# Other start addresses in SBUF for the split weights, half of x's blocks and the down weights

## The chip, the cores and the metric

The kernel runs on one core of a Trainium2 chip. The metric is the device time of one execution in microseconds. The kernel before was run three times: 998.46, 1000.0 and 1001.24 us, median 1000.0. A further execution was taken with the hardware profiler; every profile line below comes from it.

## The reference

One decoder-like block: cross attention onto a context, then a mixture of eight experts in which every expert is computed for every token. All is float32. Biases of the attention are drawn at random, so they can't be dropped.

```python
# x (16,112,256), ctx (16,375,256), Wq/Wk/Wv (256,256)
q = layernorm(x) @ Wq + bq;  k = ctx @ Wk + bk;  v = ctx @ Wv + bv
x = x + softmax(q @ k.T / 16) @ v
n = layernorm(x)                                  # 1792 tokens of 256
cw = softmax(n @ w_router) * softmax(n @ w_gating / 0.1)
cw = cw / (cw.sum(-1) + 1e-9)                     # (tokens, 8)
for e in range(8):                                # w_gate, w_up (8,256,1024), w_down (8,1024,256)
    h = silu(n @ w_gate[e]) * (n @ w_up[e])
    x = x + cw[:, e] * (h @ w_down[e])
```

## The kernel before

**Attention, then experts.** The first part, some 125 us, computes attention batch by batch in a software pipeline (attn_group, attn_batch, tick). Its result lies transposed in x1T (two halves of 896 tokens). From then on almost all time goes to the experts, in 128 steps, one for each of 8 experts, 2 token halves h, 4 column groups j and gate or up (the list steps, L440). The order of instructions on TensorE, VectorE, ScalarE and GpSimd is the order in which the program writes them down; nothing reorders it.

**Products.** A gate or up step multiplies a 2 x 2 block matrix of x with a 2 x 2 block matrix of the weight by seven products instead of eight (PROD, L20: the Strassen-Winograd scheme). x's seven combinations are made once per half (xs_hi and xs_lo, L121 and L122, each block 128 partitions x 448 float32r, 1792 bytes in a partition); the weight's seven are made for each step. Full float32 precision is kept by splitting every operand into a high part that float32r holds exactly and a low part. A product is then three passes (PASSES, L79): high x high, high weight x low x, low weight x high x. Function prod (L573) issues these three matmuls. The weight block is the stationary operand, which TensorE loads before the matmul; x's block is the moving operand, which streams through. The products go to the PSUM banks A, B, C and E, and VectorE combines them (L684 to L729).

**Split weights.** A step's weight is fetched by the SP queue into a raw buffer (load_raw), combined by GpSimd (load_t), rounded by ScalarE into the high half of a w buffer (load_hi, L486), and GpSimd subtracts to get the low half (load_lo, L491). A w buffer holds 2 x 7 blocks of 128 float32r, 7168 bytes in a partition, which is 28 x 256. There are eight w buffers. In the attention part the same buffers hold x, parts of the context and x1T (wide, L132).

**Down products.** The hidden values of a half are split too, into hhi and hlo (four buffers each of 3584 bytes), and multiplied with w_down: in down_group (L531) a block of the hidden values is stationary and the down weight is moving, 256 columns, again in three passes: hhi with the high weight, hhi with the low weight, hlo with the high weight. Down weights come through rawd into four buffers d (load_d, L493), each 4096 bytes: a high and a low half of 2 x 256. Function fill puts down groups between the products of the following steps, so TensorE always has one of the two at hand. gather adds finished groups to acc with the routing weight.

**Addresses.** All these tiles are taken in turn from two pools; a tile starts at the next multiple of 32 bytes. Function buf (L106) takes all rotating buffers; AHEAD (L104) puts a small unused tile ahead of the first buffer of some tags and so shifts where these start. The starts in the built program, modulo 256 bytes:

| tile | role in the experts | start modulo 256 |
|---|---|---|
| xs_hi, xs_lo | moving, products | 192 (all 28 blocks) |
| w, every block of all 8 buffers | stationary, products | 128 |
| d, all 4 buffers | moving, down products | 0 |
| hhi / hlo | stationary, down products | 64 / 192 |

All blocks inside these tiles begin at multiples of 256 bytes from the tile's start (448 x 4 = 7 x 256; 128 x 4 = 2 x 256), so a tile's residue is that of each of its operands.

The names that return below: L578 is the matmul of a product, L544 that of a down group, L276, L305, L332 and L342 are matmuls of the attention.

Of the kernel before, what the change touches and what calls it, by code (L numbers as in the profile page):

```python
# [8 lines left out]
F32 = mybir.dt.float32  # L9
FR = mybir.dt.float32r  # L10
# [21 lines left out]
def kernel(  # L32
# [18 lines left out]
    P = 128  # L51
    B, TQ, D = x.shape
# [9 lines left out]
    NH = 2  # L62
    HT = NT // NH
    HB = B // NH
    N = HT // 2
# [5 lines left out]
    cpool = ctx.enter_context(tc.tile_pool(name="const", bufs=1))  # L71
    fpool = ctx.enter_context(tc.tile_pool(name="ffn", bufs=2))
# [28 lines left out]
    BUFS = {"w": 8, "d": 4, "hhi": 4, "hlo": 4, "s": 11, "v1": 2, "raw": 3, "rawd": 2, "tt": 2, "y": 3}  # L101


    AHEAD = {"w": 16, "d": 32, "hhi": 16, "hlo": 32}  # L104

    def buf(tag, shape, name, dtype=F32):  # L106
        if tag in AHEAD:
            fpool.tile([P, AHEAD.pop(tag)], F32, tag=f"ahead_{tag}", name=f"ahead_{tag}", bufs=1)
        return fpool.tile(shape, dtype, tag=tag, name=name, bufs=BUFS[tag])

    zero = buf("y", [P, 256], "zero")
    nc.vector.memset(zero, 0.0)
    zero = zero.bitcast(mybir.dt.bfloat16)
# [4 lines left out]
    warm = cpool.tile([P, G], F32, name="warm")  # L118
    nc.scalar.activation(warm, nhalf, AF.Exp)

    xs_hi = [[cpool.tile([P, N], FR, name=f"xs_hi{h}{i}") for i in range(7)] for h in range(NH)]  # L121
    xs_lo = [[cpool.tile([P, N], FR, name=f"xs_lo{h}{i}") for i in range(7)] for h in range(NH)]  # L122
    pairs = [(h, b, min(2, NTT - 2 * b)) for h in range(NH) for b in range((NTT + 1) // 2)]
    accs = {(h, b): cpool.tile([P, n, D], F32, name=f"acc{h}{b}") for h, b, n in pairs}
    acc = [accs[h, b][:, i, :] for h, b, n in pairs for i in range(n)]
# [4 lines left out]

    WF = 2 * 7 * P
    wide = [buf("w", [P, WF], f"wide{i}") for i in range(7)]  # L132
    qk_b = [wide[0][:, i * KC * GT : (i + 1) * KC * GT] for i in range(2)]
    late = [wide[i] for i in (3, 1, 2)]
# [4 lines left out]
    x1T = [wide[5 + h].rearrange("p (k t) -> p k t", k=KC) for h in range(NH)]  # L139

    wn = buf("d", [P, 2, KC, D], "wn")
    wT = buf("d", [P, 2, KC, D], "wT")
    wv_b = buf("d", [P, 2, KC, D], "wv_b", FR)
# [3 lines left out]
    b_b = buf("rawd", [P, 2, D], "b_b")  # L147
    wv = buf("rawd", [P, KC, D], "wv")
    bk_c = spool.tile([P, KC], F32, tag="bk_c", name="bk_c", bufs=1)
    junk = cpool.tile([P, D], F32, name="junk")  # L150
    bkb = buf("y", [P, D], "bkb").rearrange("p (k q) -> p k q", k=KC)

    xg = {}
# [351 lines left out]
    for k in range(NW):  # L505
        e, i = divmod(k, PER)
        if e == 0:
            n = i - 2
            plan(n - 1, "raw", k)
        else:  # L510
            n = 2 * PER * (e - 1) + PER + (2, 4, 6, 7, 8, 10, 12, 13)[i]
# [4 lines left out]
    for q in range(E * NJ):  # L516
        e, j = divmod(q, NJ)
        n = 2 * j + 1 if e == 0 else 2 * PER * (e - 1) + PER + 2 * j + 7
# [393 lines left out]
```

## Time and profile before

| what | value |
|---|---|
| median of three runs | 1000.0 us (998.46 to 1001.24) |
| the profiled execution | 1002.6 us |
| its span, from the first to the last instruction | 1000.8 us |
| mean granted TensorE clock | 0.986 of full speed |
| matmuls of products (L578) / of down groups (L544) | 2688 / 2688 |
| SBUF bytes of one partition used by the last tile's end | 228668 |

The profile page gives busy time by engine, a chain of work followed back from the last instruction, and groups of equal instructions. "PE" is TensorE's matmuls, "PEld" its loads of stationary operands, "DVE" VectorE, "ACT" ScalarE, "POOL" GpSimd. A matmul's duration on the page reaches from its start to its modelled end; matmuls are pipelined and overlap, so the time that one costs is read from the start of one to the start of the next in the view in order of time. In that view the columns are start in us, length of the merged entry in us, engine, line, operation, out<-in by names, shape, and how many instructions were merged.

### The profile page before, as it was taken

To read this page: it belongs to the slowest core of one execution; us is meant where nothing else is said; L and a number is where in the kernel's file an instruction comes from. 1 tells how busy PE (TensorE), PEld (TensorE's weight loads), DVE (VectorE), ACT (ScalarE), POOL (GpSimd) and SP (SyncE) were. 2 spreads that over 40 slices of the span, in tenths; PEclk is the share of its full clock that TensorE was granted. 3 is DMA by queue.
4 is the path that set the end of the run, shared out by engine and by line. 5 is a ranking of instruction groups with operands and counts; after the bars stand their busy time and mean duration, and the time that the engine had idled before them with its cause. 6 is when DMAs were issued, how large, how long until landed. Compare 5 with 4: busy or idle time off the path is not lost.

```text
span 1000.8 us, 16367 instructions
## 1 busy us (share of the span) xinstructions
PE 978.5 (98%) x6052; PEld 911.8 (91%) x6052; DVE 802.9 (80%) x1529; ACT 496.1 (50%) x1036; POOL 419.4 (42%) x548
## 2 busy tenths in 40 slices
PE   7989889999999999999999999999999999999998
PEld 4867778999999999999999999999999999999998
DVE  5875668888888888878888888888887888788786
ACT  4554664445545554455444553555444554455342
POOL 2352765245615462255414460555235632445000
PEclk9999979999999999999999999999999999999999
DMA  9710111001100110011100110011001110010011
GB/s 222 208 29 14 41 47 53 11 23 53 40 14 22 44 34 31 12 28 48 43 2 23 53 54 1 22 44 43 22 12 42 37 40 11 22 43 2 1 38 38
DMA packets 36736, 39.06 MB, mean 39 GB/s; under 512 B 3552, under 2 KB 34656, under 8 KB 36656
## 3 DMA queue, kind: packets, MB, share of 16 engines
q1 hardware_dynamic: 36384, 37.76, 13.0%
q8 instruction: 47, 0.77, 0.3%
q14 instruction: 33, 0.27, 0.1%
q10 hardware_dynamic: 272, 0.26, 0.1%
HBM read 34.34 MB, written 1.84 MB: 36 GB/s over the span
## 4 chain that ended last, share of the span: by engine, by line
PE 93%; DVE 2%; DMA 2%; ACT 1%; POOL 0%; issue 0%; SPq 0%; DVEq 0%
PE pd L544 32%; PE pC L578 16%; PE pA L578 15%; PE pB L578 15%; PE pE L578 8%; PE ps_s L305 2%; PE ps_aT L332 1%; PE ps_o L342 1%; DMA wide<-in_x_dram 1%; PE ps_qk L276 1%; PE ps_lg L406 1%; DMA ctx<-in_ctx_dram 1%; PE ps_cT L298 1%; PE ps_pT L323 0%; ACT xs_hi L380 0%; PE ps_x1T L369 0%
## 5 line engine op out<-in xcount | busy, mean ns | idle before, releaser
L544 PE MATMUL pd<-wd,hhi 128*128 128x256 f32 x1792 | 338.8, 280 | 0.0
L544 PEld LDWEIGHTS pd<-wd,hhi 128*128 128x128 f32 x1792 | 308.9, 188 | 14.1
L544 PE MATMUL pd<-wd,hlo 128*128 128x256 f32 x896 | 250.6, 280 | 0.0
L578 PE MATMUL pC<-xs_hi,w 128*128 128x448 f32 x512 | 189.7, 370 | 0.8 <-DVE s_3c L707 0.8
L578 PE MATMUL pB<-xs_hi,w 128*128 128x448 f32 x512 | 188.6, 368 | 0.0
L578 PE MATMUL pA<-xs_hi,w 128*128 128x448 f32 x512 | 187.4, 366 | 0.9 <-ACT v L679 0.4
L544 PEld LDWEIGHTS pd<-wd,hlo 128*128 128x128 f32 x896 | 169.3, 189 | 0.0
L561 POOL TENSOR_TENSOR acc<-acc,y 128x256 f32<-128x256 f32 x45 | 35.9, 824 | 247.5 <-ACT y L560 247.5
L491 POOL TENSOR_TENSOR w<-raw,w 128x384 fp32r<-128x384 f32 x64 | 73.2, 1144 | 136.1 <-ACT w L486 136.1
L679 ACT COPY v<-pA 128x448 f32<-128x448 f32 x128 | 68.2, 533 | 92.2 <-PE pA L578 92.2
L578 PEld LDWEIGHTS pC<-xs_hi,w 128*128 128x128 f32 x512 | 96.8, 189 | 11.3 <-DVE s_3c L707 1.1
L578 PEld LDWEIGHTS pB<-xs_hi,w 128*128 128x128 f32 x512 | 97.1, 190 | 5.6
L578 PEld LDWEIGHTS pA<-xs_hi,w 128*128 128x128 f32 x512 | 96.6, 189 | 5.9 <-ACT v L679 1.0
L578 PE MATMUL pC<-xs_lo,w 128*128 128x448 f32 x256 | 93.6, 366 | 0.0
L578 PE MATMUL pE<-xs_hi,w 128*128 128x448 f32 x256 | 93.4, 365 | 0.0
L578 PE MATMUL pB<-xs_lo,w 128*128 128x448 f32 x256 | 93.1, 364 | 0.0
L578 PE MATMUL pA<-xs_lo,w 128*128 128x448 f32 x256 | 92.7, 362 | 0.0
L491 POOL TENSOR_TENSOR w<-tt,w 128x512 fp32r<-128x512 f32 x64 | 83.5, 1304 | 2.1
L496 POOL TENSOR_TENSOR wd<-rawd,wd 128x512 fp32r<-128x512 f32 x32 | 41.7, 1302 | 72.6 <-ACT wd L495 72.6
L578 PEld LDWEIGHTS pE<-xs_hi,w 128*128 128x128 f32 x256 | 48.2, 188 | 3.2
L578 PEld LDWEIGHTS pC<-xs_lo,w 128*128 128x128 f32 x256 | 48.5, 189 | 1.5
L578 PEld LDWEIGHTS pB<-xs_lo,w 128*128 128x128 f32 x256 | 48.3, 189 | 1.7
(1779 smaller groups left out, 1887.4 us busy)
## 6 DMA issues: line engine op xcount, KB each, us to landing
raw<-in_L_ffn_w_gate_dram SPq DMA_DIRECT2D x32, 256.0 KB, 3.3
raw<-in_L_ffn_w_up_dram SPq DMA_DIRECT2D x32, 256.0 KB, 2.7
rawd<-in_L_ffn_w_down_dram SPq DMA_DIRECT2D x32, 256.0 KB, 2.6
ctx<-in_ctx_dram SPq DMA_DIRECT2D x13, 336.0 KB, 6.8
wide<-in_x_dram SPq DMA_DIRECT2D x4, 448.0 KB, 4.0
out_dram<-acc SPq DMA_DIRECT2D x6, 256.0 KB, 2.2
wide<-in_ctx_dram SPq DMA_DIRECT2D x3, 336.0 KB, 7.0
ctx<-in_ctx_dram SPq DMA_DIRECT2D x13, 39.0 KB
```

The lines of the kernel that those rows point to most:

```text
L276: nc.tensor.matmul(ps, m_sb[:, k, m * P : (m + 1) * P], xnT[:, k, :], start=(k == 0), stop=(k == KC - 1),)
L298: nc.tensor.transpose(ps[:, c * KT : (c + 1) * KT], ct[:, c, k * P : (k + 1) * P], ident[:KT, :KT])
L305: nc.tensor.matmul(sc, qkT[g][:, k, i * TQ : (i + 1) * TQ], ctT[k], start=(k == 0), stop=(k == KC - 1),)
L332: nc.tensor.matmul(ps[:, k, :], ct[:, c, k * P : (k + 1) * P], pT[:, c, :], start=(c == 0), stop=(c == NK - 1),)
L342: nc.tensor.matmul(po, aT[:, a, k, :], (wv_hi, wv_lo)[w][:, k, :], start=(k == 0 and s == 0), stop=(k == KC - 1 and s == 2),)
L406: nc.tensor.matmul(ps[:, j, :], x1T[h][:, k, j * P : (j + 1) * P], wr[:, k, :], start=(k == 0), stop=(k == KC - 1),)
L491: nc.gpsimd.tensor_sub(wts[k][1][:, d], w, f(wts[k][0][:, d]))
L496: nc.gpsimd.tensor_sub(t[:, 1], rawds[q], f(t[:, 0]))
L544: nc.tensor.matmul(pd, hs[a][:, t * P : (t + 1) * P], wds[q][w][:, fi, :], start=(opening and s == 0), stop=(last and s == 2), skip_group_ ...
L561: nc.gpsimd.tensor_add(acc[tt], acc[tt], y)
L578: nc.tensor.matmul(ps, w_[w][:, wi, :], (xs_hi, xs_lo)[a][h][xi], start=(start and s == 0), stop=(stop and s == 2), skip_group_check=True,)
L679: nc.scalar.copy(v1, pa)
```

## The change

Only addresses change. Buffers of tag w are taken 8 elements (32 bytes) longer and used from element 4 (16 bytes) on; with the length of 7200 bytes each next buffer starts 32 bytes further modulo 256. Buffers of tag d are taken 16 elements (64 bytes) longer. AHEAD is set so that the eight used w starts are 16, 48, 80, 112, 144, 176, 208 and 240, and the four d starts 0, 64, 128 and 192 modulo 256. x's blocks are now taken half by half, with an unused tile of 32 bytes ahead of the second half: 192 for half 0, 224 for half 1. The starts of hhi and hlo stay at 64 and 192. To have room, the scratch tile junk goes; what is written there goes to the last block of acc, which is filled later. acc, cw, wr and the y buffers move by 32 bytes as a consequence.

```diff
-    AHEAD = {"w": 16, "d": 32, "hhi": 16, "hlo": 32}
+    AHEAD = {"w": 40, "d": 0, "hhi": 16, "hlo": 32}
+    LONGER = {"w": (8, 4), "d": (16, 0)}

     def buf(tag, shape, name, dtype=F32):
-        if tag in AHEAD:
+        if AHEAD.get(tag):
             fpool.tile([P, AHEAD.pop(tag)], F32, tag=f"ahead_{tag}", name=f"ahead_{tag}", bufs=1)
-        return fpool.tile(shape, dtype, tag=tag, name=name, bufs=BUFS[tag])
+        if tag not in LONGER:
+            return fpool.tile(shape, dtype, tag=tag, name=name, bufs=BUFS[tag])
+        n = 1
+        for d in shape[1:]:
+            n *= d
+        more, first = LONGER[tag]
+        t = fpool.tile([shape[0], n + more], dtype, tag=tag, name=name, bufs=BUFS[tag])[:, first : first + n]
+        if len(shape) == 3:
+            return t.rearrange("p (a b) -> p a b", a=shape[1])
+        if len(shape) == 4:
+            return t.rearrange("p (a b c) -> p a b c", a=shape[1], b=shape[2])
+        return t
...
-    xs_hi = [[cpool.tile([P, N], FR, name=f"xs_hi{h}{i}") for i in range(7)] for h in range(NH)]
-    xs_lo = [[cpool.tile([P, N], FR, name=f"xs_lo{h}{i}") for i in range(7)] for h in range(NH)]
+    xs_hi, xs_lo = [], []
+    for h in range(NH):
+        if h:
+            cpool.tile([P, 8], F32, name="ahead_x")
+        xs_hi.append([cpool.tile([P, N], FR, name=f"xs_hi{h}{i}") for i in range(7)])
+        xs_lo.append([cpool.tile([P, N], FR, name=f"xs_lo{h}{i}") for i in range(7)])
...
-    junk = cpool.tile([P, D], F32, name="junk")
+    junk = acc[-1]
```

## The prediction

> **What bounds the kernel now.** I read the page's busy shares first, then its chain, then the stretches by engine, then TensorE's instructions in order of time.
>
> ```profile
> PE 978.5 (98%) x6052; PEld 911.8 (91%) x6052; DVE 802.9 (80%) x1529; ACT 496.1 (50%) x1036; POOL 419.4 (42%) x548
> PE 93%; DVE 2%; DMA 2%; ACT 1%; POOL 0%; issue 0%; SPq 0%; DVEq 0%
> ```
>
> The chain that ended last is 93% TensorE. The stretches (columns: PE busy, weight loads, VectorE, ScalarE, GpSimd, granted clock, DMA share, GB/s) say it more sharply:
>
> ```profile
> 250.00:500.00 250.00, 250.00 (x1560) 237.88 (x1559) 207.41 (x355) 126.85 (x250) 113.50 (x139) 1.00 0.11 31
> 500.00:750.00 250.00, 250.00 (x1561) 238.13 (x1560) 207.42 (x357) 123.40 (x243) 101.45 (x126) 1.00 0.09 27
> ```
>
> From 250 to 985 us TensorE is never idle, the clock is 1.00, and the view of waits lists nothing for it. So only the length of a matmul itself can move the time. In order of time, one gate or up step runs from one first product to the next:
>
> ```profile
> 504.66 0.36 PE L578 MATMUL pA<-xs_hi,w 128*128 128x448 f32 x1
> ...
> 506.81 0.36 PE L578 MATMUL pA<-xs_hi,w 128*128 128x448 f32 x1
> 507.01 0.36 PE L578 MATMUL pA<-xs_lo,w 128*128 128x448 f32 x1
> 507.21 0.36 PE L578 MATMUL pA<-xs_hi,w 128*128 128x448 f32 x1
> 507.41 0.36 PE L578 MATMUL pE<-xs_hi,w 128*128 128x448 f32 x1
> ...
> 508.01 0.40 PE L544 MATMUL pd<-wd,hhi 128*128 128x256 f32 x2
> 508.25 0.28 PE L544 MATMUL pd<-wd,hlo 128*128 128x256 f32 x1
> 508.36 0.40 PE L544 MATMUL pd<-wd,hhi 128*128 128x256 f32 x2
> ...
> 511.37 0.36 PE L578 MATMUL pA<-xs_hi,w 128*128 128x448 f32 x1
> ```
>
> Durations overlap, so the starts count. A step is 511.37 - 504.66 = 6.71 us: 21 product matmuls (448 columns, one every 0.20 us) and 21 down matmuls (256 columns, three in 0.35 us). Over 250 to 985 us the means of the start-to-start times are 201.7 ns (26 hiccups over 240 ns left out) and 118.0 ns; 21 x 201.7 + 21 x 118.0 = 6.71 us. Two lines of the attention stage give floors:
>
> ```profile
> 90.86 1.67 PE L276 MATMUL ps_qk<-wide,mix 128*128 128x448 f32 x4
> 69.47 1.50 PE L332 MATMUL ps_aT<-pT,wide 125*128 125x112 f32 x12
> ```
>
> ps_qk streams plain float32 at half rate: (1.67 - 0.54)/3 = 377 ns for 448 columns, so about 188 ns at the full rate of the float32r products (estimate: half). ps_aT streams so few columns that its weight loads set the pace: (1.50 - 0.28)/11 = 111 ns per load. The products therefore carry 201.7 - 188 = 13.7 ns each over the floor, the down matmuls 118.0 - 111 = 7 ns over the weight load. With 2688 of each that is 37 + 19 = 56 us in which TensorE is busy but neither waits for an engine nor streams at its own rate.
>
> That excess hangs on addresses and on phase, not on other engines. Of 110 steps that start after 250 us, 97 last 6.713 us within 2 ns, whatever VectorE, ScalarE, GpSimd and the DMAs do meanwhile; the other 13 are 0.2 us longer. Within a step the product intervals repeat by position: 200.8 ns for the first pass of most products, 197.5 for their second, on xs_lo, 209.2 for the last pass of pB's second product. All of these have the same start residues modulo 256: moving x at 192, stationary w at 128. The down matmuls (moving 0) take 117.3 ns when a hidden block at 64 is loaded next and 119.4 when one at 192 is.
>
> **What the Trainium skill says.** "TensorE: Matmul & The Clock Gate", section "Back-to-back issue gap", gives N / 2.4 + 2.5 ns. For two passes over 448 columns that is 375.8 ns, and ps_qk agrees (377); for float32r it would be 189 and 109 ns, and the trace disagrees (201.7, 118.0). "SBUF — State Buffer", section "Who interferes with whom", gives TensorE two independent read ports and says it never waits on anyone; the 56 us above speak against taking this as free. The same page's box on cachelines ("Door 1: The DMA port swizzle") names 16-byte lines, so a shift by 16 bytes changes lines; and "Operand start alignment" says its own findings are about legality, not speed. No run here shows a start at an odd multiple of 16.
>
> **The change, part by part.** In the built program all engines issue the same instructions in the same order with the same semaphore waits; only addresses differ, and the 19 VectorE instructions that wrote junk write acc[-1] instead. So nothing is queued behind anything new.
>
> - *Split weights* (w) go from residue 128 in all eight buffers to 16, 48, 80 ... 240; *x* stays at 192 in half 0 and goes to 224 in half 1. The distance w minus x, one value now (192 modulo 256) wherever a w block is loaded while x streams, becomes eight values, the odd multiples of 16. The trace holds no such distance, so I bound it. Best case: all excess goes, 2688 x 13.7 = 37 us less. Worst case: every product takes the longest interval seen, 209.2, so 2688 x 7.5 = 20 us more. The value taken: the present single distance is a special one (whole multiples of 64 on both sides, so both streams cross line and block borders in step, and a meeting repeats), and mixing should bring the mean to about the best common interval that is seen now, 198. That is 3.6 ns x 2688 = 9.7 us less.
> - *Down weights* (d) go from residue 0 to 0, 64, 128, 192 against hidden blocks still at 64 and 192. Both hidden kinds then see all four distances. ps_o, the attention matmul of this form (256 columns, moving at 0), has medians of 115.5 to 117 ns at distances 0, 64 and 128, beside 118.0 here. I take 0.5 ns less, 2688 x 0.5 = 1.3 us; bounds: all at the 111 floor (19 us less) or all at 122, the slow end seen (11 us more).
> - *Other engines.* ScalarE (L486) and GpSimd (L491, 1.14 and 1.30 us) write w off 32-byte borders. Cover: GpSimd is 42% busy and idles 136 us before L491 for ScalarE; a tenth slower would cost it 16 us of idle time and TensorE nothing. If that cover went, the first product of a step would wait for its low part. VectorE's tiles acc and y shift by 32 bytes: nothing taken.
> - *Start-up.* The first x load (4.12 us, first on the chain) lands in a w buffer, now 16 bytes off. Bound: 0 to twice its time, 4 us more. I take 0.
> - *junk to acc[-1]*: the same engine in the same order, and acc[-1] is filled long after: 0.
>
> Sum: -9.7 - 1.3 = -11.0 us. The profiled execution lasted 1002.6 us (span 1000.8), so 991.6; it lies 2.6 above the median of the three runs, 1000.0, so against that median 989 us.
>
> **Rivals.**
> 1. *Large gain:* an offset of half a 32-byte pair keeps the two read streams apart throughout. Two thirds of the products' excess and a fifth of the downs' go: 24.6 + 3.8 = 28 us, 972 us. For it: the excess is large and follows addresses only. Against: the weight load advances at another rate than the moving stream (111 ns for 128 columns, 188 for 448), so a start offset alone can't part them for good.
> 2. *No difference:* because the streams drift past each other, start residues average out and intervals stay near 201 and 118: 998 to 1003 us. For it: the down matmuls differ by only 2 ns between distances 64 and 192. Against: the same drift repeats to the ns in 97 steps, so starts do decide.
> 3. *Slower:* blocks that start inside a 64-byte unit touch one unit more per weight load and, in half 1, per moving row, and meet more often. It decides once the products' mean is 1.1 ns up (3 us). At half of the way to the longest interval seen (+3.5 ns) it costs 9.4 us: 1009 us. For it: the present layout puts x, w and both hidden kinds on distinct multiples of 64, which may be a good point already. Against: the products carry more excess than anything else, so that point isn't good for them.
> 4. *It doesn't do what it says:* excluded; the built addresses have the residues named.
>
> **How the numbers follow.** Main case 0.55 (own range 979 to 996), rival 1 0.15, rival 2 0.12, rival 3 0.18. Half of rival 1 falls below 972, and rather over half of rival 3 above 1008, about 0.17 together: the range is 972 to 1008. A measurement of this kernel can tell about 0.3%, 3 us. Faster: main and rival 1 less the shallow end of the main case, 0.69; same: 0.12 and a little of the main case and rival 3, 0.14; slower: 0.17.
>
> **What would show it.** Right: product intervals near 198 ns, a step length that now differs from step to step and repeats with the eight weight buffers, TensorE still without waits between 250 and 985 us, the start of the first pass of the experts unmoved. Down intervals near 117.5, differing with the d buffer. Wrong: product intervals above 202 (rival 3), intervals unchanged (rival 2), or TensorE waiting for VectorE, 80% busy now, if TensorE gains so much that it runs ahead (the 13 longer steps would then grow). If the attention stage alone moved, my reading of where the addresses act would be wrong.

## The result and the profile after

| | before | after |
|---|---|---|
| median of five runs | 1001.24 us (998.46 to 1002.89) | 1005.59 us (1004.88 to 1007.59) |
| profiled execution / its span | 1002.6 / 1000.8 us | 1005.97 / 1004.2 us |
| first product starts at (from the trace's start times) | 112.7 us | 112.7 us |
| mean start to start, product / down matmul, 250 to 985 us | 201.73 / 118.04 ns | 203.76 / 117.76 ns |
| steps without a wait (95 after 250 us in each) | 6.713 to 6.714 us | 6.711 to 6.787 us |

After over before, worked out from all five executions of each, is 1.0051, with a 95% interval of 1.0031 to 1.0071: the change makes the kernel 0.5% slower. (The two medians alone give 1.0043.) The means and step lengths here and below are worked out from the start times of the trace; product intervals above 240 ns, which hold a wait, are left out of the means.

The busy shares on the page of the changed kernel:

```profile
PE 982.0 (98%) x6052; PEld 910.9 (91%) x6052; DVE 804.1 (80%) x1529; ACT 496.0 (49%) x1036; POOL 419.8 (42%) x548
```

The instruction counts and the shares of the chain (93% TensorE) are those of before; only TensorE's busy time grew, by 3.5 us, and the span by 3.4. The stretches of the changed kernel (columns as before: PE, weight loads, VectorE, ScalarE, GpSimd, clock, DMA share, GB/s):

```profile
250.00:500.00 250.00, 250.00 (x1554) 236.73 (x1553) 207.43 (x353) 126.09 (x250) 113.66 (x139) 1.00 0.10 31
500.00:750.00 250.00, 250.00 (x1555) 236.86 (x1554) 206.41 (x354) 122.40 (x241) 101.55 (x125) 1.00 0.09 27
```

By its busy time TensorE is still never idle, at a clock of 1.00, but it starts 1554 and 1555 matmuls where it started 1560 and 1561. Busy time can't show this loss; only the count and the start times do. One step of the changed kernel, in order of time (half 1, x at 224, w at 48):

```profile
505.80 0.37 PE L595 MATMUL pA<-xs_hi,w 128*128 128x448 f32 x1
...
508.18 0.37 PE L595 MATMUL pA<-xs_lo,w 128*128 128x448 f32 x1
508.39 0.37 PE L595 MATMUL pA<-xs_hi,w 128*128 128x448 f32 x1
508.59 0.37 PE L595 MATMUL pE<-xs_hi,w 128*128 128x448 f32 x1
...
509.20 0.40 PE L561 MATMUL pd<-wd,hhi 128*128 128x256 f32 x2
...
509.56 0.40 PE L561 MATMUL pd<-wd,hhi 128*128 128x256 f32 x2
...
510.27 0.36 PE L595 MATMUL pB<-xs_hi,w 128*128 128x448 f32 x1
...
512.54 0.37 PE L595 MATMUL pA<-xs_hi,w 128*128 128x448 f32 x1
```

L595 and L561 are the old L578 and L544. The step is 512.54 - 505.80 = 6.74 us. Step lengths now repeat with period 16, the eight w buffers times the two halves. Product matmuls start 0.20 or 0.21 us after one another, where they started 0.20 us apart.

In 13 of the steps TensorE does wait, before and after. The busy time of its matmuls hides it; the waits of its weight loads (PEld) show it. At pC's first product the load waits for the VectorE instruction that reads bank C (the source line c12 = w16 + pc). The view has 13 such lines for each kernel between 250 and 985 us (us in total, times, longest); one of before and the same one of after:

```profile
PEld pC L578 <- DVE s_63w L729: 0.3, 1, 0.3
PEld pC L595 <- DVE s_63w L746: 0.2, 1, 0.2
```

The account of the change: products 2.03 ns x 2688 = +5.5 us; down matmuls -0.28 x 2688 = -0.8; the excess of the product intervals over 240 ns, all at such a wait, falls from 2.4 us (26 of them) to 1.2 (13), -1.2. Together that is +3.5 us, beside +3.4 in the spans.

### The profile page after: what moved, and what is told of

The parts are those of the page before. It is cut to its first block, busy times and chain, and to the rows that moved or that the text cites. A ratio compares the mean times of both kernels' runs of the same rounds, so it can differ in the third digit from the quotient of the medians.

```text
span 1004.2 us, 16367 instructions
## 1 busy us (share of the span) xinstructions
PE 982.0 (98%) x6052; PEld 910.9 (91%) x6052; DVE 804.1 (80%) x1529; ACT 496.0 (49%) x1036; POOL 419.8 (42%) x548
## 4 chain that ended last, share of the span: by engine, by line
PE 93%; DVE 2%; DMA 2%; ACT 1%; POOL 0%; issue 0%; SPq 0%; DVEq 0%
PE pd L561 31%; PE pC L595 16%; PE pA L595 16%; PE pB L595 15%; PE pE L595 8%; PE ps_s L322 2%; PE ps_aT L349 1%; PE ps_o L359 1%; DMA wide<-in_x_dram 1%; PE ps_qk L293 1%; PE ps_lg L423 1%; DMA ctx<-in_ctx_dram 1%; PE ps_cT L315 1%; PE ps_pT L340 0%; ACT xs_hi L397 0%; PE ps_x1T L386 0%
## 5 line engine op out<-in xcount | busy, mean ns | idle before, releaser
L561 PE MATMUL pd<-wd,hhi 128*128 128x256 f32 x1792 | 338.9, 280 | 0.0
L561 PEld LDWEIGHTS pd<-wd,hhi 128*128 128x128 f32 x1792 | 308.5, 188 | 15.8
L561 PE MATMUL pd<-wd,hlo 128*128 128x256 f32 x896 | 250.9, 280 | 0.0
L595 PE MATMUL pC<-xs_hi,w 128*128 128x448 f32 x512 | 189.8, 371 | 0.8 <-DVE s_3c L724 0.8
L595 PE MATMUL pA<-xs_hi,w 128*128 128x448 f32 x512 | 189.1, 369 | 0.7 <-ACT v L696 0.4
L595 PE MATMUL pB<-xs_hi,w 128*128 128x448 f32 x512 | 188.0, 367 | 0.0
L561 PEld LDWEIGHTS pd<-wd,hlo 128*128 128x128 f32 x896 | 168.7, 188 | 0.1
L578 POOL TENSOR_TENSOR acc<-acc,y 128x256 f32<-128x256 f32 x45 | 36.1, 831 | 249.2 <-ACT y L577 249.2
L508 POOL TENSOR_TENSOR w<-raw,w 128x384 fp32r<-128x384 f32 x64 | 73.2, 1144 | 136.7 <-ACT w L503 136.7
L595 PEld LDWEIGHTS pC<-xs_hi,w 128*128 128x128 f32 x512 | 96.9, 189 | 10.8 <-DVE s_3c L724 1.1
L595 PEld LDWEIGHTS pA<-xs_hi,w 128*128 128x128 f32 x512 | 96.9, 189 | 6.3 <-ACT v L696 1.0
L595 PEld LDWEIGHTS pB<-xs_hi,w 128*128 128x128 f32 x512 | 96.8, 189 | 6.1
L595 PE MATMUL pB<-xs_lo,w 128*128 128x448 f32 x256 | 94.1, 368 | 0.0
L595 PE MATMUL pA<-xs_lo,w 128*128 128x448 f32 x256 | 94.1, 368 | 0.0
L595 PE MATMUL pC<-xs_lo,w 128*128 128x448 f32 x256 | 94.1, 367 | 0.0
L595 PE MATMUL pE<-xs_hi,w 128*128 128x448 f32 x256 | 93.7, 366 | 0.0
L508 POOL TENSOR_TENSOR w<-tt,w 128x512 fp32r<-128x512 f32 x64 | 83.0, 1297 | 2.8
L595 PEld LDWEIGHTS pE<-xs_hi,w 128*128 128x128 f32 x256 | 48.2, 188 | 4.2
L595 PEld LDWEIGHTS pB<-xs_lo,w 128*128 128x128 f32 x256 | 48.3, 189 | 2.1
L595 PEld LDWEIGHTS pC<-xs_lo,w 128*128 128x128 f32 x256 | 48.4, 189 | 1.8
```

What stands on the lines that cost most here:

```text
L508: nc.gpsimd.tensor_sub(wts[k][1][:, d], w, f(wts[k][0][:, d]))
L561: nc.tensor.matmul(pd, hs[a][:, t * P : (t + 1) * P], wds[q][w][:, fi, :], start=(opening and s == 0), stop=(last and s == 2), skip_group_ ...
L578: nc.gpsimd.tensor_add(acc[tt], acc[tt], y)
L595: nc.tensor.matmul(ps, w_[w][:, wi, :], (xs_hi, xs_lo)[a][h][xi], start=(start and s == 0), stop=(stop and s == 2), skip_group_check=True,)
```

## The experiments

A product's **distance** below is the start of the stationary block that is loaded next minus the start of the moving block, modulo 256. All nine full kernels are the changed one with other values of AHEAD and LONGER, and with x at 192 throughout unless x is named. For x at 192 the unused tile ahead of the second half goes, with the line `if h:` over it, which the cuts below leave out. Every ratio is to the kernel before on the same chip and is worked out from all executions, so it can differ from the ratio of the medians by up to 0.1%. The means in ns are of one profiled execution each.

| kernel | w; d; hhi/hlo | ratio [95%] | product, down ns | first-order change, us |
|---|---|---|---|---|
| before | 128; 0; 64/192 | 1 | 201.73, 118.04 | |
| after | odd multiples of 16, x 192 and 224; 0, 64, 128, 192; 64/192 | 1.0051 [1.0031, 1.0071] | 203.76, 117.76 | +5.5 - 0.8 |
| w_alone | odd multiples of 16; 0; 64/192 | 1.0015 [1.0005, 1.0025] | 203.92, 116.72 | +5.9 - 3.5 |
| d_alone | 128; 0, 64, 128, 192; 64/192 | 0.9987 [0.9975, 1.0] | 201.45, 117.56 | -0.8 - 1.3 |
| x_alone | 128, x 192 and 224; 0; 64/192 | 1.001 [0.9997, 1.0024] | 202.77, 117.08 | +2.8 - 2.6 |
| w_spread_32 | multiples of 32; 0; 64/192 | 1.0021 [1.0011, 1.0031] | 203.55, 117.43 | +4.9 - 1.6 |
| w_at_96 | 96; 0; 64/192 | 0.9974 [0.9965, 0.9984] | 203.90, 115.19 | +5.8 - 7.7 |
| best_distances | 128; 64; 128/128 | 0.999 [0.998, 0.9999] | 201.19, 118.03 | -1.5 - 0.0 |
| hlo_at_64 | 128; 0; 64/64 | 0.9917 [0.9894, 0.994] | 200.49, 115.41 | -3.3 - 7.1 |
| best_step | 128; 192; 128/128 | 0.9894 [0.9875, 0.9913] | 200.03, 114.87 | -4.6 - 8.5 |
| best_step_b | 128; 192; 128/0 | 0.9838 [0.9814, 0.9862] | 200.04, 113.37 | -4.5 - 12.6 |

The last column is the difference of each mean to before, times 2688; it leaves out the waits.

**The three parts alone.** w_alone leaves out the shift of x and the spread of d:

```diff
-    AHEAD = {"w": 40, "d": 0, "hhi": 16, "hlo": 32}
-    LONGER = {"w": (8, 4), "d": (16, 0)}
+    AHEAD = {"w": 48, "d": 0, "hhi": 16, "hlo": 32}
+    LONGER = {"w": (8, 4)}
-            cpool.tile([P, 8], F32, name="ahead_x")
```

> The kernel before with the eight w buffers at 16, 48 ... 240 modulo 256 (the residue of each buffer as in the changed kernel); x stays at 192, d at 0, hidden blocks at 64 and 192. Theory A, the products became slower because of w's new starts: product intervals 203.5 to 204 ns (201.7 before), down intervals 118.0, step mean 6.76 us, 4 to 6 us over the kernel before. Theory B, the new starts of x or d, or the mixture of all, did it: product intervals within 0.5 ns of 201.7 and the time within 1.5 us of the kernel before.

The products rose by 2.19 ns, about as much as under the whole change, as theory A said. The down matmuls, whose own addresses are those of before, fell by 1.32 ns, which neither theory had: what a down matmul costs depends on what ran before it too. So the kernel became only 0.15% slower, 1.5 us where theory A had 4 to 6.

d_alone spreads only d:

```diff
+    AHEAD = {"w": 16, "d": 32, "hhi": 16, "hlo": 32}
+    LONGER = {"d": (16, 0)}
-            cpool.tile([P, 8], F32, name="ahead_x")
```

> The kernel before with the four d buffers at 0, 64, 128, 192; w at 128, x at 192 as before. Theory A: product intervals 201.7 ns as before, down intervals 117.5 to 117.8 (118.0 before), 0.5 to 1.5 us less than the kernel before. Theory B, that moving d upsets the products that follow the downs: product intervals 202.5 ns or more, 2 us or more slower.

The kernel became 0.13% faster, at the edge of what can be told, as theory A said; the down matmuls fell by 0.48 ns. This part alone isn't what cost time.

x_alone moves only x's second half:

```diff
+    AHEAD = {"w": 8, "d": 32, "hhi": 16, "hlo": 32}
+    LONGER = {}
```

> The kernel before with x's second half at 224 instead of 192; w at 128, d at 0. Theory A, start residues average out in the products unless w moves: steps of half 1 as long as those of half 0, 6.71 us, no change in time. Theory B, the 32 bytes of x matter: steps of half 1 differ from those of half 0 by 0.03 us or more (64 such steps: 2 us or more).

The two halves make a comparison inside one execution. From product to product the interval is 201.03 ns in half 0 (distance 192) and 204.05 ns in half 1 (distance 160); the stationary blocks are the same. Yet a step of half 1 lasts 6.720 us against 6.713, since the down matmuls fell again. Theory A is wrong about the products, and theory B's 0.03 us a step didn't come; the time is that of before within its interval.

The parts don't add up. Alone they cost 0.15%, -0.13% and 0.10%, together 0.12%; the whole change costs 0.51%. By the last column they give +0.5 us together against +4.7. The products' rise is there with w alone, but the fall of the down matmuls that comes with it (-3.5 us with w alone) is nearly lost when all three move (-0.8).

**TensorE by itself.** streams has no other work than matmuls on one moving and one stationary tile. Here go issues ten matmuls of N columns with the moving block at m and the stationary block at s; cols is the number of stationary columns:

```diff
+MOV = (0, 32, 64, 128, 192)
+STAT = tuple(range(0, 256, 16))
...
+    for N in (448, 256):
+        for m in MOV:
+            for s in STAT:
+                go(N, m, s)
+    for cols in (128, 64, 32):
+        for m, s in ((192, 128), (192, 16), (0, 64), (0, 0)):
+            go(448, m, s, cols, 16)
...
```

> Nothing of the reference is computed: TensorE alone runs float32r matmuls back to back, ten of each kind, with 448 and 256 moving columns, the moving start at 0, 32, 64, 128, 192 and the stationary start at every multiple of 16 modulo 256; then the same with 128, 64 and 32 stationary columns. Theory A, two reading streams that drift past each other: all 80 cells for 448 columns lie within 196 to 210 ns, with no distance below 194, and with 32 stationary columns the interval falls to about 190. Theory B, a distance that keeps the streams apart exists: some cells near 189 while others are over 205, in a pattern by stationary minus moving start. Theory C, the excess comes from other engines: every cell near 189.

Intervals for 448 columns with the moving block at 0, from the start times; each is the mean of the last seven of a group's nine:

```
distance   0     16    32    48    64    80    96    112
ns       203.3 206.6 204.6 203.6 201.7 203.6 200.1 203.6
distance  128   144   160   176   192   208   224   240
ns       202.7 202.4 205.7 204.4 200.1 203.9 206.6 203.4
```

Only the distance counts: with the moving block elsewhere the values belong to the same distances within 1.2 ns. All 80 groups lie between 199.6 and 206.7 ns, in theory A's range; nothing is near 189, so the excess neither comes from other engines (theory C) nor goes away at some distance (theory B). The 192 of the kernel before is, with 96, the lowest value. The mean over the odd multiples of 16, which the change spreads the products over, is 203.9 ns; the changed kernel's mean is 203.76. And 160 against 192, which x_alone saw as 204.05 against 201.03, is here 205.7 against 200.1. So the table gives the direction, but not the size: the products took 201.73 ns before, not 200.1, and it is partly luck that 203.76 meets the table so closely. With 256 columns the groups span 113.3 to 120.7 ns, and there one distance can settle at two values: 192 takes 117.7 ns with the moving block at 0 and 113.4 with it at 128. One part of theory A missed: with 32 stationary columns the 448-column interval stays at 202 to 206 ns. So the excess isn't the length of the weight load, though that changes which distance is low (192 takes 205.8 ns with 32 stationary columns).

**Is it the start off 32 bytes?** w_spread_32 puts the buffers at all multiples of 32:

```diff
+    AHEAD = {"w": 48, "d": 0, "hhi": 16, "hlo": 32}
+    LONGER = {"w": (8, 0)}
-            cpool.tile([P, 8], F32, name="ahead_x")
```

> Only w is moved: the eight buffers at 0, 32, 64 ... 224, so no start is off 32 bytes. Theory A2, each product costs what its distance (stationary minus moving start, modulo 256) costs in the table of the bare streams, and only the mean over the distances counts: the table's mean over the multiples of 32 is 203.1 ns, so product intervals 202.5 to 203.6, between the kernel before (201.7) and w alone on odd multiples of 16 (203.9). Theory B2, starts off 32 bytes are what costs: product intervals 201.7 or less, as before.

It costs as much as w_alone, with no block off a 32-byte border. The mean of the table over multiples of 32 is 203.1 ns; the products took 203.55, in theory A2's range. So it isn't the odd 16 bytes that cost.

**Do the distances add up?** w_at_96 gives all products one distance that isn't among the low ones (96 - 192 = 160), which by the table alone makes the kernel slower:

```diff
+    AHEAD = {"w": 8, "d": 40, "hhi": 16, "hlo": 32}
+    LONGER = {}
-            cpool.tile([P, 8], F32, name="ahead_x")
```

> Only w is moved, all eight buffers together from 128 to 96, so the common distance to x becomes 160 instead of 192. Theory A2: the table has 205.7 ns there against 200.1, so product intervals rise to 204 to 206 and the kernel takes 6 to 11 us more, twice the change's loss, though no buffer differs from another. Theory B2, that it is the mixture of distances or the odd multiples of 16 that costs: no change, 201.7.

The products took 203.90 ns, just under the forecast 204 to 206, with no mixture and no odd 16 bytes: a single other distance costs the products as much as the spread over eight. But the time forecast missed: the kernel became faster, by 2.8 us. In order of time (w_at_96; L559 is the down matmul, L593 the product):

```profile
500.12 0.39 PE L559 MATMUL pd<-wd,hhi 128*128 128x256 f32 x2
...
500.46 0.39 PE L559 MATMUL pd<-wd,hhi 128*128 128x256 f32 x2
...
504.21 0.37 PE L593 MATMUL pB<-xs_lo,w 128*128 128x448 f32 x1
504.42 0.37 PE L593 MATMUL pB<-xs_hi,w 128*128 128x448 f32 x1
```

The products are slower, 0.21 us here. But three down matmuls take 0.34 us instead of the 0.35 of before, though d, hhi and hlo stand where they stood before: -7.7 us against +5.8. hlo_at_64 changes nothing but hlo's start:

```diff
+    AHEAD = {"w": 16, "d": 32, "hhi": 16, "hlo": 0}
+    LONGER = {}
-            cpool.tile([P, 8], F32, name="ahead_x")
```

> Only hlo is moved, from 192 to 64, so all hidden blocks lie 64 past d. Theory A2: the table has 113.3 ns for 256 columns at distance 64, so down intervals fall from 118.0 to 113.5 to 115, products stay at 201.7, 8 to 12 us less. Theory C2, that the downs keep drifting through several patterns because products stand between them: down intervals 116.5 to 118, less than 4 us gained.

The kernel became 0.8% faster, 8.3 us, with steps of 6.633 us. The gain is theory A2's, but only part of the reason is: the down matmuls took 115.41 ns, just above its range, and the products, which it left at 201.7, fell to 200.49. best_distances takes for each pair the distance that the table calls best:

```diff
+    AHEAD = {"w": 16, "d": 48, "hhi": 16, "hlo": 0}
+    LONGER = {}
-            cpool.tile([P, 8], F32, name="ahead_x")
```

> x 192, w 128 as before; d 64, both hidden kinds 128: every pair that meets has a distance with the table's lowest value (w on x and hidden on x 192: 200.1 ns; hidden on d and w on d 64: 113.3). Theory A2: products 200.1 to 201, downs 113.5 to 114.5, step 6.60 to 6.63 us, 985 to 989 us. Theory C2: downs 116 or more, 994 us or more.

The forecast gain of 12 to 16 us didn't come: the time is that of before within 0.1%, and the down matmuls took 118.03 ns, as before. A table of steady pairs doesn't price a mixed sequence.

**The whole step, by itself.** steps issues the kernel's 42 matmuls of a step in their order, on tiles with given starts, with nothing else running. A layout in CONFIGS is the starts of w, d, hhi and hlo with x at 0. Each is issued three times (REPS), 256 layouts in multiples of 64 among them:

```diff
+    def step(W, D, *H):
+        prod("A", 1, True, False, W)
+        prod("B", 6, True, True, W)
+        prod("C", 5, True, False, W)
+        down(D, H)
...
+    for c in CONFIGS:
+        for _ in range(REPS):
+            step(*c)
```

> Nothing of the reference is computed. TensorE alone issues a step's 42 matmuls (21 product passes, 21 down passes, in the kernel's order and shapes) three times for each of many choices of the starts of w, d, hhi and hlo against x; no other engine works and nothing waits. First four choices: the distances of the kernel before, of hlo at 64, of the best distances, of w at 96. Theory D, TensorE's own streams set every interval and the step as a whole falls into a fixed pattern: the third repeat takes 6.713, 6.633, 6.703 and 6.700 us within 0.01, as in the full kernels. Theory E, other engines' SBUF traffic carries part of it: steps here are 0.05 us or more shorter, and the order of the four differs. Ahead of that, 448 and other column counts with 128 and 32 stationary columns[...]; and plain float32 at 448 columns, 376 ns at every start if the half rate leaves room for both streams.

In their second and third repeats the bare steps of the layouts of before, hlo_at_64, best_distances and w_at_96 last 6.713, 6.633, 6.702 to 6.706, and 6.700 to 6.701 us. In the full kernels they last 6.713, 6.633, 6.701 to 6.705, and 6.700. The trace of steps in order of time, first a step with the starts of the kernel before, then one with the best found:

```profile
201.70 0.76 PE L72 MATMUL A<-xs,w 128*128 128x448 f32 x3
...
205.05 1.22 PE L72 MATMUL D<-d,h 128*128 128x256 f32 x9
206.11 0.78 PE L72 MATMUL B<-xs,w 128*128 128x448 f32 x3
...
208.41 0.76 PE L72 MATMUL A<-xs,w 128*128 128x448 f32 x3
...
4425.09 0.76 PE L72 MATMUL A<-xs,w 128*128 128x448 f32 x3
...
4428.43 1.18 PE L72 MATMUL D<-d,h 128*128 128x256 f32 x9
4429.45 0.76 PE L72 MATMUL B<-xs,w 128*128 128x448 f32 x3
...
4431.67 0.76 PE L72 MATMUL A<-xs,w 128*128 128x448 f32 x3
```

The first step takes 6.71 us and the second 6.58, and nine down matmuls take 1.06 us and 1.02. At the third repeat the 256 layouts go from 6.580 to 6.836 us with a mean of 6.729: the kernel before already stood a little better than the mean. (30 of the 256 still change by more than 5 ns from the second repeat to the third.) The same run swept the columns. With 32 stationary columns 128 moving columns take 60 ns and 512 take 232, so each further column costs 0.45 ns. A plain float32 matmul leaves two records in the trace; each took 375.9 ns for 448 columns, 0.84 ns a column, at all 16 distances. At this half rate the addresses don't matter.

steps_mix does the same for the changed kernel: 16 successive steps with its own starts. An entry of MIX is w, x, d for each of the step's seven down groups, and (hhi, hlo), on the scale where x of half 0 is 0:

```diff
+    MIX = [(112, 0, [0, 0, 0, 0, 0, 0, 128], (128, 0)), ...]
+    for _ in range(3):
+        for c in MIX:
+            mixed(*c)
```

> Nothing of the reference is computed. TensorE alone issues sixteen consecutive steps of the changed kernel, each matmul with the start residues that it has there, three times over; then more choices of uniform starts at multiples of 32 and 16. Theory D: the second and third pass show the step lengths of the changed kernel's profile, step by step, between 6.71 and 6.80 us with a mean near 6.755 (the two steps of sixteen that also wait there left out). Theory E: the lengths differ from the changed kernel's, or are all near 6.71.

Bare steps of the second pass in ns, and below them the changed kernel's own, from 451.6 us on, in the same order:

```
bare    6715  6744 6751 6759 6743 6772 6748  6768 6745 6787 6772 6711 6729 6770 6751 6769
kernel  6795* 6744 6751 6759 6743 6772 6848* 6768 6745 6787 6772 6711 6729 6770 6751 6769
```

The starred steps hold a wait for VectorE; the other 14 agree to the ns. The step shown above of the changed kernel, here bare (trace of steps_mix in order of time):

```profile
184.89 0.78 PE L73 MATMUL A<-xs,w 128*128 128x448 f32 x3
...
188.30 1.23 PE L73 MATMUL D<-d,h 128*128 128x256 f32 x9
189.37 0.77 PE L73 MATMUL B<-xs,w 128*128 128x448 f32 x3
...
191.64 0.57 PE L73 MATMUL A<-xs,w 128*128 128x448 f32 x2
```

Here the down groups, B and the next A come 3.41, 4.48 and 6.75 us after the first A. In the changed kernel they come 3.40, 4.47 and 6.74 us after 505.80. The bare mean of 6.752 us against 6.713 is 0.039 us, times 128 steps +5.0 us: that is the products' and down matmuls' share of the loss (5.5 - 0.8 = 4.7), made by TensorE alone. Between the bare steps only the starts of its two operands differ.

The same run tried 220 more choices of uniform starts, in multiples of 16 and 32; none was shorter than 6.580 us.

**Better than both.** best_step takes the 6.580 us layout in which hhi and hlo start alike:

```diff
+    AHEAD = {"w": 16, "d": 16, "hhi": 48, "hlo": 0}
+    LONGER = {}
-            cpool.tile([P, 8], F32, name="ahead_x")
```

> All starts uniform again, chosen by the shortest fixed pattern that TensorE alone showed: x 192, w 128 as before, d 192, both hidden kinds 128. Theory D, TensorE's own streams set the step: 6.58 us a step as there, 128 x 0.133 = 17 us less than the kernel before, 981 to 986 us, ratio 0.981 to 0.986. Theory E: 990 us or more.

The kernel is 1.1% faster, but the forecast missed: 990.99 us lies in the range of theory E. Its steps come in two lengths, 6.580 and 6.673 us, with the same addresses. The length changes only at steps with a wait, at ten of the thirteen. That doesn't speak for other engines' traffic: steps_mix, where TensorE is alone, has this layout twice, once at 6.673 us and once at 6.580. best_step_b differs in hlo's start alone:

```diff
+    AHEAD = {"w": 16, "d": 16, "hhi": 48, "hlo": 32}
+    LONGER = {}
-            cpool.tile([P, 8], F32, name="ahead_x")
```

> As best_step, but hlo at 0 (64 in the scale where x is 0), the other choice whose bare step settled at 6.58 us. Theory F, whether a layout stays in its short pattern depends on the layout: every step that does not wait lasts 6.58 to 6.59 us, product intervals near 200, downs near 114.5, 983 to 988 us. Theory G, any layout with two patterns is thrown into the longer one by each waiting step: a share of the steps at 6.66 us or more, as in best_step (6.58 and 6.67), 989 to 993 us.

As theory F said, it takes 986.14 us (983.15 to 987.75, four executions) against 1001.53, 1.6% faster than before, and every step without a wait lasts 6.580 us. Its TensorE in order of time:

```profile
500.56 0.36 PE L593 MATMUL pA<-xs_hi,w 128*128 128x448 f32 x1
...
501.76 0.39 PE L559 MATMUL pd<-wd,hhi 128*128 128x256 f32 x2
...
502.78 0.36 PE L593 MATMUL pB<-xs_hi,w 128*128 128x448 f32 x1
...
507.14 0.36 PE L593 MATMUL pA<-xs_hi,w 128*128 128x448 f32 x1
```

From pA's second product to the next one it is 6.58 us; nine down matmuls take 1.02 us, as bare. Two of its stretches, and one of the 13 waits of its weight loads:

```profile
250.00:500.00 250.00, 249.82 (x1588) 238.11 (x1587) 212.18 (x360) 126.93 (x250) 112.69 (x139) 1.00 0.11 31
750.00:985.00 235.00, 231.61 (x1488) 221.04 (x1486) 195.50 (x336) 112.68 (x221) 79.70 (x96) 1.00 0.09 28
PEld pC L593 <- DVE s_63w L744: 0.4, 1, 0.4
```

TensorE starts 28 matmuls more than before in the first stretch. It is now idle for 0.18 us there and for 3.4 us in the other, part of which is the shorter kernel's end. VectorE is what comes next: the 13 waits at pC have grown from 0.3 to 0.4 us, and a step with one is 0.33 us longer than the others, where it was 0.20. That takes back 1.6 us of the 17.1 in the table.

## Why the prediction was wrong

**The step that failed is the products' term:** "mixing should bring the mean to about the best common interval that is seen now, 198. That is 3.6 ns x 2688 = 9.7 us less." It measured +2.03 ns, +5.5 us: the sign was wrong. (201.7 - 198 is 3.7, a slip that doesn't matter.) The reason given was that "the present single distance is a special one"; special it was, but it is, with 96, the lowest of the sixteen (200.1 ns), and the sixteen span only 200 to 207. From one distance in the trace I judged the value of the others. And 198 is the interval of one pass at its place in the step, not the mean of any distance: no steady group of the bare run is below 199.6 ns, so neither 198 as a mean nor the floor of 188 was within reach by these starts.

**Down matmuls.** The forecast was -0.5 ns, -1.3 us; -0.28 ns, -0.8 us was measured, and -0.48 ns for this part alone. With d alone the number is right. In the whole change it is near by luck: it was worked out from d and the hidden blocks alone, and a down matmul's time moved by 0.6 to 2.9 ns when only w or x moved. That one part changes the price of another is a term that the prediction doesn't have.

**What bounds the kernel.** This was right in the main: the excess follows addresses and not other engines, as the bare steps show more sharply than the argument did. But the view of waits was read for the matmuls alone. The 13 longer steps, left unexplained, are those in which a weight load waits for VectorE.

**Costs set to nothing.** The start of the first product stayed at 112.7 us. The first x load took 4.55 us in place of 4.12 on the chain, within its bound. GpSimd's writes of w's low part off 32-byte borders take 1144 and 1297 ns, 1144 and 1304 before. junk cost nothing that shows.

**The rivals.** Rival 3 (slower) named the right outcome, and its sign of the prediction being wrong, product intervals above 202 ns, came: it decides from 1.1 ns up, and 2.03 came, where it priced 3.5. Its argument that the present layout may be a good point was right for the products. Its mechanism fell: it blamed blocks that start inside a 64-byte unit, but in the bare runs a stationary start at 96, inside such a unit, takes 200.1 ns with the moving block at 0, as low as any, and 32 with 96 (both inside) takes 201.9 where 0 with 64 takes 201.7. The distance counts, not the unit. Rival 2 held that starts average out; that is half true, since the products of the mix come out at the average of the table, but the kernel before wasn't at the average. Rival 1 has no support: no distance brings the products near the 192.6 ns that two thirds of the excess would leave.

**The signature** came as announced: step lengths that differ and repeat with the buffers, and no new wait. It showed where the change acts, not which way. TensorE waiting longer for VectorE once it gains, which the prediction also named, came in best_step_b.

**The skill's pages.** In the Trainium skill's "TensorE: Matmul & The Clock Gate", section "Back-to-back issue gap", the formula N / 2.4 + 2.5 ns is that of an isolated matmul; for a sustained stream the section has about 131 ns at N = 512. Estimated by the formula, twice 448 columns take 375.8 ns, and a record of plain float32 in the bare run took 375.9 at every start. For float32r it would be 189.2 ns, and no steady group has less than 199.6; 512 columns of float32r in a stream took 227 to 234 ns. So for float32r neither figure of the page holds, and the measurement decides. The skill's "SBUF — State Buffer", section "Who interferes with whom", gives TensorE two independent read ports; at half rate that agrees with the runs, at full rate the time depends on how the two streams' starts stand to each other, so there too the measurement decides. Which structure in TensorE or SBUF does this stays open; the weight load's length is excluded by the 32-column runs.

## What to carry to other kernels

Where TensorE is busy without a gap, count its starts: the busy share hides an excess that only start-to-start times show. A bare kernel that issues the same sequence of matmuls on tiles with chosen start addresses gave the full kernel's step to within a few ns for six layouts and for the mix, so hundreds of layouts can be priced in one execution of 5 ms before one is built in. Two limits showed: a layout can have two lengths, of which the bare steps may show only one, and the waits for other engines aren't in it. Price the whole repeated sequence, never pairs: here pairs forecast +6 us or more where -2.8 came, and a gain where none came. And look at the waits of the weight loads beside those of the matmuls.

## What the runs showed of the hardware

- Back-to-back float32r matmuls of 448 columns take 199.6 to 206.7 ns, by the distance of the two operands' starts modulo 256 (streams), and in a bare step of 42 the start addresses alone make 6.580 to 6.836 us, 3.9% (steps).
- That excess is there with 32 stationary columns as with 128 (202 to 206 ns, streams), and no dependence on the start is seen for plain float32 (375.9 ns a record at all 16 distances, steps).
- It has a memory: matmuls with unchanged addresses changed their time by up to 2.9 ns on average when their neighbours' addresses changed (w_at_96), and one layout has two stable step lengths, 6.580 and 6.673 us (best_step).
- By columns, bare, 128 stationary (steps): 128 and 192 columns both take 111 to 112 ns (the weight load sets the pace), 256 columns 117.6 to 120, 512 columns 227 to 234. With 32 stationary columns 128 moving ones take 60 ns.
- Matmuls that are busy without a gap can hide a wait: a weight load waited 0.28 us for VectorE in 13 steps of the kernel before, each 0.20 us longer than the others.
